# Layernorm channel sums by partition-folding DMAs and 64x64 matmul tiles, with halves abreast, in a transformer and ConvNeXt block kernel

## The chip, the core and the metric

The kernel runs on one core of one Trainium2 chip. A time is the device time of one execution in microseconds (us). The kernel before has a median of 3377.36 us over three runs (3374.6 to 3380.21). The profile is one further execution, recorded by the hardware profiler: that run took 3374.66 us, of which the profile's span covers 3372.8 us. Engines are named as in the profile: PE is TensorE, PEld its weight loads, DVE VectorE, ACT ScalarE, POOL GpSimd, SP SyncE.

## What is computed

Eight images of 384 channels and 32x32 = 1024 tokens, all float32, pass through two layers. In short form:

```python
# layer 0, per image: x is (1024 tokens, 384 channels)
xn  = layernorm(x, g1, beta1, eps=1e-5)            # ln1, over the channels
q, k, v = split(xn @ w_qkv.T + b_qkv)              # 8 heads of 48
x1  = x + concat(softmax(q k^T / sqrt(48)) v) @ w_proj.T + b_proj
xn2 = layernorm(x1, g2, beta2, eps=1e-5)           # ln2
x2  = x1 + gelu(xn2 @ w_fc1.T + b_fc1) @ w_fc2.T + b_fc2     # 384 -> 1536 -> 384
# layer 1, per image
y   = depthwise_conv_7x7(x2) + dw_b
y   = layernorm(y, ln_w, ln_b, eps=1e-6)           # ln3, over the channels
y   = gelu(y @ w1 + b1)                            # 384 -> 1536
gx  = sqrt(sum over tokens of y^2); nx = gx / (mean(gx) + 1e-6)
y   = grn_gamma * (y * nx) + grn_beta + y
out = x2 + y @ w2 + b2                             # 1536 -> 384
```

## The kernel before

**Layout.** Activations lie with channels on the partitions: an image is three tiles of 128 channels by 1024 tokens, and nearly every matmul has 512 tokens (half an image, "half 0" and "half 1") as its moving side. A layernorm is over channels, and so over the three tiles and over the 128 partitions of each.

**A layernorm** is the generator `layernorm` (L366). It works on one half: DVE adds the three channel tiles into one tile `a` of 128x512 (L379, L380); one PE matmul with a 128x128 tile of ones (L383) sums over the partitions and puts the sum on all 128 rows of a PSUM bank at once; three DVE operations subtract the mean (L387); ACT squares (L392); DVE adds the squares (L396, L397); a second matmul with ones (L400) gives the variance; ACT makes the reciprocal root (L408, L409); three DVE operations scale (L412). A float32 matmul is two passes of the array, so the profile counts each as two instructions. The `yield`s between the steps are waits of a planner, told of next.

**Order.** The program is written under a manual schedule: each engine executes its own queue in the order in which `main` (L1236 to L1387) writes it. The object `flow` keeps a clock of PE work as it is written (`flow.pe(us)`, 0.857 us for a 128x512 float32 matmul). Side chains, such as a layernorm, are generators started with `flow.spawn`; each `yield` gives the PE time after which the chain's next step is written. So a layernorm's steps fall between the matmuls of other work, and a `yield` that is too short for what precedes it leaves PE waiting at the layernorm's matmul, because everything later on PE is queued behind it.

**Stages of one image in the steady part**, about 407 us of PE time: `qk`; `attention`, 64 steps of a score and a product group, each of four 64-row tiles of the array; fc1 (384 to 1536) for half 0 and half 1; fc2 (1536 to 384) by `by_thirds` (L693), a fast block product of 15 products of four matmuls instead of 18; then, for the image before this one, `grn_up` (w1), the values of the next image, and `grn_down` (w2, `by_thirds` again). The 7x7 convolution runs on DVE the whole time.

**Where the layernorms are.** ln2 half 0 is spawned in the second half of attention (L593), right after the projection of half 0, with `spaced=True`; ln2 half 1 in the middle of fc1 (L679). At the start of fc2, `next_norms` (L1285) finishes the convolution and spawns ln3 of the image before as `abreast` (L414): both halves go step by step together, in `by_thirds`, with the yields stretched by 1.4. The second half takes its tiles from the four slots of `attn`, which is idle then. ln1 of the next image is spawned by `both` (L428), half 0 and then half 1, yields stretched by 1.8, 24 us after ln3 and so mostly in `grn_up`. Image 0 has its ln1 at the very start (L1243), and the last image has fc2 by halves and its ln3 in parts (L1310).

**POOL and its DMAs.** In `by_thirds` the function `adding` (L734) adds one 512 KB tile pair to another by an accumulating DMA issued from POOL (L736), and `difference` (L656) makes e tiles in the same way (L659). They are nearly all that POOL issues in the steady part. Weights stream on SP's queue.

## Time and profile before

| engine | busy us | share of span |
|---|---|---|
| PE (matmul) | 3323.2 | 99% |
| PEld (weight load, beside PE) | 1424.9 | 42% |
| DVE | 2551.5 | 76% |
| ACT | 1422.2 | 42% |
| POOL | 155.7 | 5% |

PE is busy in nearly all of the span, so what is between 3323.2 and 3372.8 us is start, end and a few waits. The granted PE clock is 0.996 of full speed on average. The sixteen DMA engines carry 275.79 MB, 82 GB/s on average, but unevenly: a `by_thirds` stage of an image in the middle (1401.38 to 1458.03 us) shows a DMA share of 0.66, the `grn_up` after it (to 1516.40 us) 0.33, and a piece of attention (1693 to 1700 us) 0.02. In those three pieces DVE is busy 48.40 of 56.65 us, 39.55 of 58.37 us and 6.96 of 7.00 us.

The page's rows for the groups of instructions give the line, the engine and operation, output and input tile, then the count, the busy time in us, the mean in ns, and the idle time before them with what ended it.

### The profile page before, as it was taken

The numbers are of one execution on the slowest core, as the hardware profiler recorded it, in microseconds if no ns is written. First come the engines' busy times: TensorE is split into PE (matmuls) and PEld (weight loads), VectorE is DVE, ScalarE is ACT, GpSimd is POOL, SyncE is SP. The second block draws the span as 40 slices with busy tenths as digits, with TensorE's granted clock in tenths as the row PEclk, the third lists the DMA queues.
The fourth block names the chain that finished last, engine by engine and source line by source line (L and its number), as shares of the span: only waits on it lengthen the run. The fifth ranks groups of instructions, "written<-read, shape, count | busy, mean of one in ns | idle before, by whom it ended". The sixth has DMA issues, their size and how long they took to land.

```text
span 3372.8 us, 36885 instructions
## 1 busy us (share of the span) xinstructions
PE 3323.2 (99%) x14122; PEld 1424.9 (42%) x14122; DVE 2551.5 (76%) x3089; ACT 1422.2 (42%) x1868; POOL 155.7 (5%) x181
## 2 busy tenths in 40 slices
PE   8999999999999999999999999999999999999999
PEld 3334434443344433444334443344434443344455
DVE  3345798877877878779787796976888779979950
ACT  2542353444534354343543525436254352531631
POOL 0202000000000000100001000010000000000000
PEclk9999999999999999999999999999999999999999
DMA  3427101542025410435005250052501633023231
GB/s 105 132 93 199 57 18 45 160 105 63 17 68 142 112 50 17 96 120 135 21 13 126 92 139 15 14 144 83 131 14 32 168 74 103 17 56 89 61 94 53
DMA packets 146024, 275.79 MB, mean 82 GB/s; under 512 B 34224, under 2 KB 36656, under 8 KB 145456
## 3 DMA queue, kind: packets, MB, share of 16 engines
q1 hardware_dynamic: 114416, 201.13, 19.3%
q0 software_dynamic: 30848, 69.74, 10.6%
q8 instruction: 114, 1.87, 0.2%
q10 hardware_dynamic: 576, 2.48, 0.2%
q14 instruction: 70, 0.57, 0.1%
HBM read 181.52 MB, written 33.82 MB: 64 GB/s over the span
## 4 chain that ended last, share of the span: by engine, by line
PE 83%; DVE 14%; DMA 1%; ACT 1%; issue 1%; SPq 0%; POOL 0%; DVEq 0%; ACTq 0%; POOLq 0%
PE s L547 12%; PE o L567 12%; PE fc L344 12%; PE fc_p L351 10%; PE h L351 10%; PE qk L331 6%; DVE acc L847 5%; PE v L476 4%; PE o L950 4%; PE proj L490 3%; PE o_p L351 3%; DVE wqkv L847 3%; PE h_last L994 2%; DVE y L727 1%; PE ln_var L400 1%; PE qk_last L344 1%
## 5 line engine op out<-in xcount | busy, mean ns | idle before, releaser
L847 DVE SCALAR_TENSOR_TENSOR acc<-pad,vec,acc 128x1024 f32<-128x1024 f32 x1008 | 1230.1, 1274 | 0.0
L556 ACT ACTIVATE p<-s 128x1024 f32<-128x1024 f32 x512 | 523.5, 1024 | 390.4 <-PE s L547 390.0
L547 PE MATMUL s<-qk 48*64 48x512 f32 x4096 | 537.4, 593 | 1.7 <-ACT qk L450 1.5
L567 PE MATMUL o<-p,v 64*64 64x512 f32 x4096 | 531.2, 590 | 0.0
L344 PE MATMUL fc<-xn,fc 128*128 128x512 f32 x1152 | 501.7, 593 | 1.2 <-DVE x L667 1.2
L344 PEld LDWEIGHTS fc<-xn,fc 128*128 128x128 f32 x1152 | 217.8, 190 | 278.5 <-issue 270.8
L351 PE MATMUL fc_p<-hid,fc 128*128 128x512 f32 x728 | 320.3, 592 | 0.0
L895 DVE TENSOR_TENSOR y<-h,y 128x512 f32<-128x512 f32 x288 | 198.4, 691 | 113.0 <-PE h L351 102.3
L351 PE MATMUL o_p<-y,w 128*128 128x512 f32 x624 | 274.4, 596 | 6.3 <-DVE y L727 6.3
L567 PEld LDWEIGHTS o<-p,v 64*64 64x64 f32 x4096 | 157.2, 133 | 285.3 <-issue 280.2
L363 ACT ACTIVATE hid<-fc,bfc_f 128x512 f32<-128x512 f32 x192 | 130.9, 686 | 348.2 <-PE fc L344 348.1
L547 PEld LDWEIGHTS s<-qk 48*64 48x64 f32 x4096 | 152.1, 133 | 295.6 <-issue 272.6
L351 PEld LDWEIGHTS fc_p<-hid,fc 128*128 128x128 f32 x728 | 138.3, 190 | 174.1 <-issue 169.3
L331 PE MATMUL qk<-xn,wqkv 128*128 128x512 f32 x480 | 207.4, 592 | 0.0
L351 PE MATMUL h<-acc,w_A 128*128 128x512 f32 x432 | 204.0, 592 | 0.0
L847 DVE SCALAR_TENSOR_TENSOR wqkv<-pad,vec,wqkv 128x416 f32<-128x416 f32 (+1 forms) x288 | 193.4, 745 | 0.6
L351 PEld LDWEIGHTS o_p<-y,w 128*128 128x128 f32 x624 | 117.8, 190 | 158.7 <-issue 128.3
L508 DVE TENSOR_TENSOR attn<-o,attn 128x512 f32<-128x512 f32 x64 | 44.0, 687 | 137.0 <-ACT attn L506 136.9
L450 ACT ACTIVATE qk<-qk,bqk 128x1024 f32<-128x1024 f32 x40 | 44.6, 1114 | 238.7 <-PE qk L331 238.7
L331 PEld LDWEIGHTS qk<-xn,wqkv 128*128 128x128 f32 x480 | 91.1, 190 | 114.1 <-issue 113.8
L476 PE MATMUL v<-wqkv,xn 128*128 128x384 f32 x384 | 128.6, 493 | 0.6 <-DVE xn L412 0.6
L490 PE MATMUL proj<-attn,wproj_sb 128*128 128x512 f32 x288 | 127.3, 595 | 0.8 <-DVE attn L534 0.8
(271 smaller groups left out, 3194.7 us busy)
## 6 DMA issues: line engine op xcount, KB each, us to landing
w_A<-in_w SPq DMA_DIRECT2D x72, 384.0 KB, 3.2
fc<-s_fc SPq DMA_DIRECT2D x91, 256.0 KB, 2.8
hid<-hid POOLq DMA_DIRECT2D x42, 512.0 KB, 6.8
fc<-in_wfc SPq DMA_DIRECT2D x54, 384.0 KB, 5.8
w<-s_w SPq DMA_DIRECT2D x78, 256.0 KB, 2.7
y<-y POOLq DMA_DIRECT2D x36, 512.0 KB, 7.3
xn<-in_x SPq DMA_DIRECT2D x16, 768.0 KB, 7.7
x<-in_x SPq DMA_DIRECT2D x16, 768.0 KB, 6.6
```

The costliest lines, as they stand in the source:

```text
L331: nc.tensor.matmul(out=ps[:, half(h)], lhsT=lhsT(k), rhs=rhs(k)[:, half(h)], start=(k == 0), stop=(k == nk - 1),)
L344: nc.tensor.matmul(out=ps, lhsT=lhsT(k), rhs=rhs(k)[:, half(h)], start=(k == 0), stop=(k == nk - 1))
L351: nc.tensor.matmul(out=bank, lhsT=lhsT, rhs=rhs, start=k == 0, stop=k == len(pairs) - 1)
L363: nc.scalar.activation(dst, src, function, **kw)
L476: nc.tensor.matmul(out=ps[:, :C], lhsT=xn[:, k, t * P : (t + 1) * P], rhs=wv_sb[:, k, :], start=(k == 0), stop=(k == CT - 1),)
L490: nc.tensor.matmul(out=ps, lhsT=wproj_sb[:, m, ct * P : (ct + 1) * P], rhs=attn[:, m, :], start=(m == 0), stop=(m == CT - 1),)
L547: nc.tensor.matmul(out=s[64 * i : 64 * i + 64, j, :], lhsT=kT[64 * j : 64 * j + HD, m, k0 : k0 + 64], rhs=qT[64 * j : 64 * j + HD, m, half ...
L556: nc.scalar.activation(p, s, AF.Exp)
L567: nc.tensor.matmul(out=outs[i][64 * j : 64 * j + 64, :], lhsT=v[keys, t, at : at + 64], rhs=p[keys, j, :], start=(t == 0), stop=(t == KT - 1),
L847: nc.vector.scalar_tensor_tensor(dst, window, tap, dst, ALU.mult, ALU.add)
L895: nc.vector.tensor_tensor(dst, bank, part, ALU.add)
L950: nc.tensor.matmul(out=ps, lhsT=tiles[k], rhs=y(k, part), start=(k == 0), stop=(k == HT - 1))
```

## The change

A new generator `token_sums` replaces the two matmuls with the 128x128 ones. Without `fold` it does what was done before. With `fold` 0 or 1, an accumulating DMA on POOL's queue first adds one half of the partitions of the 128x512 tile to the other (64 rows of 2 KB, 128 KB), the chain yields 3.4 us, and then two matmuls with 64x64 tiles of ones bring the sum of the 64 folded rows to the output's upper and lower 64 rows. Half 0 of the tokens folds into rows 0 to 63 and half 1 into rows 64 to 127, so that two halves abreast use all four 64x64 tiles of the array. With `fold="columns"`, for a half on its own, the left 256 columns are folded into the upper rows and the right 256 columns into the lower rows (two DMAs of 64 KB); the four tiles then have 256 columns each, the two column groups get a PSUM tile each, and the three subtractions of the mean become six of half width, the Ln one becomes two.

Folding is used in ln3 of images 0 to 6 and in ln1 of images 1 to 7 (halves abreast), and in ln2 half 0 of all eight images (columns). ln1 of image 0, ln2 half 1 and the last image's own ln3 keep the full sum. ln1 of images 1 to 7 goes from `both` to `abreast` with the factor 1.8; its delay after ln3 is 28 us instead of 24 (6 for image 1 as before), and its second half takes two "p" tiles of the pool `three` as places (image 1: `attn`, as ln3 does).

```diff
-    def layernorm(src, dst, h, eps, g, name, switch, spare=False, spaced=False, slow=1.0):
+    def token_sums(t, name, fold):
+        width = t.shape[-1]
+        if fold is None:
+            total = o_tile(name)[:, :width]
+            nc.tensor.matmul(out=total, lhsT=ones, rhs=t, start=True, stop=True)
+            flow.pe(U * width / NH)
+            return [(total, slice(0, width))]
+        rows = [slice(0, 64), slice(64, P)]
+        parts = [(fold, slice(0, width))]
+        if fold == "columns":
+            parts = [(j, slice(j * width // 2, (j + 1) * width // 2)) for j in range(2)]
+        for j, cols in parts:
+            nc.gpsimd.dma_start(out=t[rows[j], cols], in_=t[rows[1 - j], cols], accum_op=ALU.add)
+        yield 3.4
+        totals = []
+        for j, cols in parts:
+            total = o_tile(f"{name}_{j}")[:, : cols.stop - cols.start]
+            for i in rows:
+                nc.tensor.matmul(out=total[i, :], lhsT=ones[rows[j], :64], rhs=t[rows[j], cols], start=True, stop=True)
+            flow.pe(U * width / NH / 2)
+            totals.append((total, cols))
+        return totals
+
+    def layernorm(src, dst, h, eps, g, name, switch, spare=None, spaced=False, slow=1.0, fold=None):
...
         yield 2.6 * slow
-        total = o_tile(f"{name}_sum{h}")[:, :width]
-        nc.tensor.matmul(out=total, lhsT=ones, rhs=a, start=True, stop=True)
-        flow.pe(U * width / NH)
+        totals = yield from token_sums(a, f"{name}_sum{h}", fold)
         yield 0.8
         for ct in range(CT):
-            nc.vector.scalar_tensor_tensor(dst[:, ct, cols], total, -1.0 / C, src[:, ct, cols], ALU.mult, ALU.add)
+            for total, part in totals:
+                to, of = dst[:, ct, cols][:, part], src[:, ct, cols][:, part]
+                nc.vector.scalar_tensor_tensor(to, total, -1.0 / C, of, ALU.mult, ALU.add)
...
         yield 1.8 * slow
-        var = o_tile(f"{name}_var{h}")[:, :width]
-        nc.tensor.matmul(out=var, lhsT=ones, rhs=squares[0], start=True, stop=True)
-        flow.pe(U * width / NH)
+        totals = yield from token_sums(squares[0], f"{name}_var{h}", fold)
         yield 0.8
...
-        nc.scalar.activation(rstd, var, AF.Ln, bias=eps, scale=1.0 / C)
+        for var, part in totals:
+            nc.scalar.activation(rstd[:, part], var, AF.Ln, bias=eps, scale=1.0 / C)
...
-    def abreast(*args, parts=(0, 1)):
-        chains = [layernorm(*args[:2], h, *args[2:], spare=(h is parts[1])) for h in parts]
+    def averages():
+        return [attn[:, i, :] for i in range(4)]
+
+    def weight_places(name):
+        tiles = [three.tile([P, 2, NH], F32, tag="p", name=f"{name}_{i}") for i in range(2)]
+        return [t[:, j, :] for t in tiles for j in range(2)]
+
+    def abreast(*args, places=averages, fold=True, factor=1.4):
+        chains = [
+            layernorm(*args[:2], h, *args[2:], spare=places if h else None, fold=h if fold else None) for h in range(2)
+        ]
...
-                yield 1.4 * max(waits)
+                yield factor * max(waits)
...
-                ln = flow.spawn(layernorm(xt, xn, 0, eps0, "g2", f"ln2_{b}", False, spaced=True))
+                ln = flow.spawn(layernorm(xt, xn, 0, eps0, "g2", f"ln2_{b}", False, spaced=True, fold="columns"))
...
-        flow.finish(abreast(xn, xn, eps0, "g1", "ln1_0", False))
+        flow.finish(abreast(xn, xn, eps0, "g1", "ln1_0", False, fold=False))
...
-                state["norm1"] = flow.spawn(
-                    after(state["norm3"], both(xn, xn, eps0, "g1", f"ln1_{b + 1}", True, slow=1.8), 24 if b else 6)
-                )
+                name = f"ln1_{b + 1}"
+                places = (lambda: weight_places(name)) if b else averages
+                norm = abreast(xn, xn, eps0, "g1", name, True, places=places, factor=1.8)
+                state["norm1"] = flow.spawn(after(state["norm3"], norm, 28 if b else 6))
```

## The prediction, made before the changed kernel had run

> **What bounds the kernel now.** I read the busy row and the chain of waits on the page, then the rows of the two layernorm matmuls, then PE's waits.

> ```profile
> PE 3323.2 (99%) x14122; PEld 1424.9 (42%) x14122; DVE 2551.5 (76%) x3089; ACT 1422.2 (42%) x1868; POOL 155.7 (5%) x181
> ...
> PE 83%; DVE 14%; DMA 1%; ACT 1%; issue 1%; SPq 0%; POOL 0%; DVEq 0%; ACTq 0%; POOLq 0%
> ...
> L400 PE MATMUL ln_var<-ln_sq,ones 128*128 128x512 f32 (+3 forms) x82 | 43.8, 617 | 10.1 <-DVE ln_sq L397 10.1
> L383 PE MATMUL ln_sum<-ln_a,ones 128*128 128x512 f32 (+3 forms) x82 | 43.0, 606 | 9.2 <-DVE ln_a L380 9.2
> ```

> PE sets the end: removed PE time is gained unless a wait takes its place. DVE's share of the chain is start and end, where the last image's convolution runs by itself. The two rows' idle time (19.3 us) is mostly image 0 (gaps of 7.40, 4.34 and 3.38 us at its first sums, before any other work); from image 2 on, the layernorms cost almost no waiting. What a full sum costs, the timeline shows. In fc2, PE's rows:

> ```profile
> 1405.67 1.02 PE L383 MATMUL ln_sum<-ln_a,ones 128*128 128x512 f32 x2
> 1406.53 1.02 PE L383 MATMUL ln_sum<-attn,ones 128*128 128x512 f32 x2
> 1407.39 2.74 PE L351 MATMUL fc_p<-hid,fc 128*128 128x512 f32 x6
> ```

> Columns: start, duration, rows merged. Starts are 0.86 us apart: 0.86 for one sum, 1.72 for a pair, like any 128x512 matmul. In attention:

> ```profile
> 1695.09 0.69 DVE L380 TENSOR_TENSOR ln_a<-ln_a,x 128x512 f32<-128x512 f32 x1
> 1695.76 1.04 PE L567 MATMUL o<-p,v 64*64 64x512 f32 x8
> 1696.73 1.12 PE L383 MATMUL ln_sum<-ln_a,ones 128*128 128x512 f32 x2
> 1697.79 1.09 PE L547 MATMUL s<-qk 48*64 48x512 f32 x8
> 1698.69 1.04 PE L567 MATMUL o<-p,v 64*64 64x512 f32 x8
> ```

> Product groups start 1.72 apart without a sum (1694.04, 1695.76), here 2.93: the sum costs 1.21, its 0.86 and 0.35 for going from four tiles to one and back. Its input was ready at 1695.78, 0.95 before PE came.

> [...] attention's group of four, x8 with its two passes, takes 0.86, as one full matmul does, and the sum between such groups costs 0.35 more than itself. [...]

> ```profile
> hid<-hid POOLq DMA_DIRECT2D x42, 512.0 KB, 6.8
> fc_e<-hid POOLq DMA_DIRECT2D x14, 512.0 KB, 5.2
> qk<-qk SPq DMA_DIRECT2D x96, 64.0 KB, 2.3
> ```

> [...] I add 0.4 us for the second of two 64 KB folds.

> **The change, part by part.**

> *PE work.* ln2 half 0: 8 images, two sums each, 16 at 1.21 before. Afterwards four tiles of 256 columns among tiles of the same shape: half of 0.86 and a little for loads, 0.45. Gain 16 x 0.76 = 12.2 us. ln3 and ln1: 7 images, two pairs each, both: 28 pairs at 1.72. Afterwards 0.86 plus the 0.35 for leaving and re-entering the full array: 1.21; gain 28 x 0.51 = 14.3. Together 26.5 us. If the 256-column groups cost as much as 0.69 each, 3.8 less.

> *Work beside PE.* 88 DMAs, 8.8 MB on 275.79, and their issue on POOL (1.18 us for each 512 KB one, surely less here; POOL is 5% busy); DVE's mean subtractions in ln2 become six half-width operations of about 0.4 instead of three of 0.68, 0.3 us more per image, beside PE since DVE is 76% busy; one more Ln on ACT (42%). All hidden; bounds 0 and 1 us for each.

> *The latency of a fold, L,* from DVE's last addition to PE's start: [...] I take 2.8, and 2.4 for 64 KB; upper end 5.2, as if size didn't matter. Behind a fold's wait on PE stands everything PE has left.

> *ln3, six images in by_thirds* (the seventh goes by halves with wider gaps: nothing). In the built program's order, t counted from fc2's start: the sum group comes after 11 matmuls (9.4 to 10.6). The convolution ended long before (DVE waits 16.6 us for this sum in the trace), so the sum's folds are free. But the third product's last matmul now follows the sum group, and DVE has two operations on that product ahead of the mean subtractions: they end at 13.0. Six subtractions of 0.61: 16.7. Then one hid addition of 1.2, two e ones of 1.2 and an x one of 0.69: 20.9. The squares' additions (2 x 0.69 a half) end at 22.2 and 23.6. POOL issues the second fold then; its two earlier 512 KB adds were issued at 13.6 and 15.3. With 2.8 it lands at 26.4. PE arrives 16 matmuls after the sum group, at 24.4, and could lose nothing only with the second half there by about then: a stall of 2.0 to 2.2. 6 x 2.1 = 12.6 us. Bounds: nothing [...], and 4.5 each, 27, at L = 5.2.

> *ln1.* Half 1's sums, squares, scaling and DMA places move forward to half 0's; the steps issue nothing on SP before or after the change, and on POOL they pass the next by_thirds' adds, which start later. With the factor 1.8 the yield of 3.4 leaves 6.1 us of PE work for a fold; DVE adds 1 to 2 us of lead, having been done 0.77 to 3.19 before PE's arrival at ln1's groups in the trace: 7 to 8 us for L = 2.8. No stall for images 2 to 7. Image 1's (delay 6) folds stand on POOL behind the hid adds of its by_thirds: 0 to 2 us, against 2.0 that its half 1 waits now (1.83 and 0.21): nothing.

> *ln2 half 0.* The sum stands four pairs of attention after the projection, at +6.9 us; DVE is done at +2.65 in the usual image, the second 64 KB fold has landed at +5.6: 1.3 to spare. The variance has 3.6 us from DVE's end to PE, and needs 2.8: 0.8 to spare. In image 1 and in image 7 DVE is late already (gaps of 0.93 and 0.47 now at the variance): stalls of 1.5 and 1.0, together 2.5.

> *Sum.* 26.5 - 12.6 - 2.5 = 11.4, less 1 us for loads and issue: 10.4. Against the span of 3372.8: 3362.4. The three unprofiled runs' median stands 4.6 above that span: **3367 us**.

> **Rivals.** *No new wait* (0.20): the squares of ln3 come early enough[...]. For it: DVE had 16.6 us of slack at the sum. Against: the order puts DVE's two operations on the third product in front. 3377.4 - 26.5 + 3 = 3354.

> *The price of switching eats the gain* (0.10): [...] at 0.85 more instead of 0.35 the 28 groups gain nothing, and with ln3's wait only about ln2's 12.2 - 2.5 - 12.6 remains: 3380, no change.

> *Small folds are slow* (0.22), the other side: a 128x2 KB accumulation has a fixed price near the 5.2 us of the fastest 512 KB one, because adding in the DMA, not moving bytes, takes the time. Place: PE at ln3's variance and both ln2 groups. ln3 loses 6 x 4.5 = 27; ln2 loses 1.6 at the sum and 2.0 at the variance (5.6 needed, 1.3 and 0.8 spare at 2.4 + 0.4), 8 x 3.6 = 29, with 2.5 for images 1 and 7. 58 against 26.5: 3377.4 + 32 = 3409. It decides from about 1.2 us above my L: ln3 20, ln2 6 to 7, the gain is gone at 4.0 for 128 KB. For it: L736's median is 6.8. Against: those run while DMA is 0.66 busy; ln2's run at a share of 0.02.

> **Chances.** My forecast 0.48, with its own range 3359 to 3376; the others as given. 0.2% is 6.8 us, about what can be told from no change here. Faster than 3370.6: 0.8 of mine, all of the first rival, a little of the second: 0.61. Within: the rest of mine, most of the second, a few hundredths of the slow one's milder forms: 0.19. Slower: 0.20. The range 3350 to 3394 leaves out part of the first rival and the upper half of the slow one.

> **What would show it.** At PE's variance matmuls of ln3 a wait of about 2 us on a DMA, six times; at ln1 none; at ln2 about none but in images 1 and 7. Attention's product groups around a sum 2.2 apart instead of 2.93. A pair's place in fc2 1.2 wide. The row of 128 KB folds from POOL near 2.8 us, of 64 KB near 2.4. Wrong would be: folds over 4 us, DVE's squares before 20, or waits on folds in ln2 of every image.

## The result, and the profile after

The changed kernel takes 3412.96 us (median of four runs, 3408.96 to 3415.62), against 3377.02 us before: a ratio of 1.0105, 95% interval 1.0087 to 1.0122. It is slower by 36 us. The forecast was 3367, and the range 3350 to 3394 did not hold it. The profiled span is 3407.2 us, 34.4 more than before.

The page's busy row and PE's largest waits in the kernel after (columns of a wait: engine, line and waiting tile, what it waited for, us in total, times, longest us; L387 is the folded sum, L373 the full one):

```profile
PE 3322.6 (98%) x14330; PEld 1413.7 (41%) x14330; DVE 2549.8 (75%) x3113; ACT 1424.5 (42%) x1876; POOL 229.1 (7%) x269
```

```profile
PE ln_var L387 <- DMA ln_sq<-ln_sq: 14.0, 11, 3.6
PE fc_p L351 <- DVE hid L762: 9.2, 6, 1.5
PE ln_var L373 <- DVE ln_sq L423: 8.7, 9, 3.4
...
PE fc_p L351 <- issue: 7.7, 7, 1.7
...
PE h L351 <- DVE y L930: 5.6, 6, 0.9
```

Three groups of waits are new, with no such row among PE's waits in the kernel before: for the folds of a variance, for DVE's `hid` tiles in by_thirds (with the "issue" row beside it), and for DVE's `y` in grn_up. PE's busy time did not fall, although work was taken away. Passes of half rate and halves that no longer run together, both seen below, are part of the reason: in the run below that has neither in fc2 ("ln3's variance later") PE is busy 3309.3 us.

Where an image gained and lost shows in the stages of one in the middle, image 3. The views are busy times by window (columns: window, length, then busy time and instructions of PE, PEld, DVE, ACT and POOL, granted PE clock, DMA share, GB/s), first before, then after; the rows are fc2, grn_up and attention.

```profile
1401.38:1458.03 56.65, 56.65 (x134) 25.08 (x132) 48.40 (x67) 15.93 (x25) 7.08 (x6) 1.00 0.66 163
1458.03:1516.40 58.37, 58.37 (x138) 25.84 (x137) 39.55 (x59) 34.42 (x47) 0.00 (x0) 1.00 0.33 113
1617.95:1737.00 119.05, 119.05 (x1031) 42.37 (x1030) 88.79 (x93) 70.29 (x75) 0.00 (x0) 1.00 0.07 17
```

```profile
1415.26:1476.02 60.76, 57.02 (x138) 23.72 (x136) 43.68 (x60) 12.24 (x19) 10.49 (x10) 0.97 0.69 160
1476.02:1536.30 60.28, 59.35 (x149) 25.25 (x148) 43.72 (x66) 38.36 (x53) 1.62 (x2) 1.00 0.35 114
1637.86:1755.35 117.49, 117.49 (x1044) 42.28 (x1043) 88.67 (x96) 70.39 (x76) 3.33 (x4) 1.00 0.10 19
```

Attention, the window of the image after it, gives 1.57 us back. fc2 takes 4.11 more and grn_up 1.91 more, 4.45 in sum. From one `qk` to the next, images 2 to 5 take 411.1, 411.9, 410.8 and 412.4 us against 407.4, so the steady image costs 4.1 us more on average and the four 16.5. Images 0 and 1 together cost 11.8, image 6 4.8 and the last one 1.3: the 34.4 us.

The fc2 stage of image 3 in PE's timeline, after (start, duration, rows merged, in brackets idle before and what ended it):

```profile
1437.07 2.74 PE L351 MATMUL fc_p<-fc_e,fc 128*128 128x512 f32 x6
1441.25 1.08 PE L387 MATMUL ln_var<-ln_sq,ones 64*64 64x512 f32 x4 [1.44 <-DMA ln_sq<-ln_sq]
1442.09 1.07 PE L387 MATMUL ln_var<-attn,ones 64*64 64x512 f32 x4
1443.09 1.92 PE L351 MATMUL fc_p<-fc_e,fc 128*128 128x512 f32 x2
1444.80 18.28 PE L351 MATMUL fc_p<-hid,fc 128*128 128x512 f32 x40
1463.85 1.95 PE L351 MATMUL fc_p<-hid,fc 128*128 128x512 f32 x4 [0.77 <-issue]
1467.33 1.98 PE L351 MATMUL fc_p<-hid,fc 128*128 128x512 f32 x4 [1.53 <-DVE hid L762]
```

Four losses can be read here, each as the distance between starts less a matmul's own time:

- PE waits for the first variance fold: 1.60 us.
- The second half's fold lands 0.84 later, so the two halves run one after the other, and the group is 1.84 long instead of 0.86: 0.98.
- The first matmul after it starts at 1443.09 and the next at 1444.80, 1.71 later instead of 0.86. Its two passes (a pass is one of a matmul's two records: the page counts 4096 for the 2048 score matmuls) and the two after them take 0.854 us each instead of 0.428: 1.70. Such half-rate passes follow this wait in three images of six. They are not lost in full: fc2 takes 60.8, 60.8 and 61.3 us in these three (1, 3 and 5) and 60.0, 59.7 and 59.8 in the others, where the late stalls told of next are longer.
- About twenty microseconds later come two stalls, 0.93 and 1.70 us, for `hid` tiles from DVE: 2.63. (The view puts the first down to issue; DVE's `hid` addition before it ended 0.1 us earlier.)

With 0.37 that the sum's group of 64x64 tiles takes over its own passes (from 1424.27 to 1428.49 us with it and seven full passes, where nine at 0.428 would take 3.85) this makes 7.3, and smaller amounts bring it to 7.6 us over the 62 matmuls' worth of work that the stage now holds. Before, it held 66: the 60 of the product, four full sums of ln3 and two of ln1's half 0, which now runs later. 7.6 less the 3.43 of the four matmuls' worth that left is the 4.1 us lost.

ACT and DVE show where the late stalls come from. In ACT's timeline, first before and then after, look at the order of the Ln and of the copy of `x` into `pad`:

```profile
1417.03 0.69 ACT L408 ACTIVATE ln_rstd<-ln_var,eps 128x512 f32<-128x512 f32 x1 [4.66 <-PE ln_var L400]
...
1436.08 0.64 ACT L663 COPY pad<-x 128x512 f32<-128x512 f32 x1 [9.88 <-DVE x L727]
```

```profile
1452.09 0.63 ACT L698 COPY pad<-x 128x512 f32<-128x512 f32 x1 [14.23 <-DVE x L762]
...
1454.04 0.69 ACT L433 ACTIVATE ln_rstd<-ln_var,eps 128x512 f32<-128x512 f32 x1
```

DVE after:

```profile
1455.42 2.08 DVE L437 SCALAR_TENSOR_TENSOR acc<-acc,vec,ln_rstd 128x512 f32<-128x512 f32 x3 [2.70 <-ACT ln_rstd L434]
1457.41 2.07 DVE L437 SCALAR_TENSOR_TENSOR acc<-acc,vec,attn 128x512 f32<-128x512 f32 x3
...
1466.06 1.22 DVE L762 TENSOR_TENSOR hid<-hid 128x1024 f32<-128x1024 f32 x1
```

Before, the Ln waited for PE alone. After, the variance is on PSUM by 1443.1, but the Ln starts at 1454.04: in ACT's queue it now stands behind the copy of `x` into `pad`, and that copy waits for DVE, whose own work waits for the product that PE's wait has delayed. DVE then stands 2.70 us at the scaling of ln3, and the `hid` additions queued behind it reach PE too late (1467.33).

### The profile page after: what moved, and what is told of

It reads as the page before. It is cut to its first block, busy times and chain, and to the rows that moved or that the text cites. A ratio compares the mean times of both kernels' runs of the same rounds, so it can differ in the third digit from the quotient of the medians.

```text
span 3407.2 us, 37644 instructions
## 1 busy us (share of the span) xinstructions
PE 3322.6 (98%) x14330; PEld 1413.7 (41%) x14330; DVE 2549.8 (75%) x3113; ACT 1424.5 (42%) x1876; POOL 229.1 (7%) x269
## 5 line engine op out<-in xcount | busy, mean ns | idle before, releaser
L582 PE MATMUL s<-qk 48*64 48x512 f32 x4096 | 547.9, 595 | 4.6 <-ACT p L591 3.1
L602 PE MATMUL o<-p,v 64*64 64x512 f32 x4096 | 542.8, 593 | 0.0
L351 PE MATMUL fc_p<-hid,fc 128*128 128x512 f32 x728 | 325.1, 602 | 16.9 <-DVE hid L762 9.2
L351 PE MATMUL o_p<-y,w 128*128 128x512 f32 x624 | 274.5, 597 | 8.0 <-DVE y L762 8.0
L351 PEld LDWEIGHTS fc_p<-hid,fc 128*128 128x128 f32 x728 | 139.6, 194 | 201.5 <-issue 179.6
L351 PE MATMUL h<-acc,w_A 128*128 128x512 f32 x432 | 207.8, 596 | 5.6 <-DVE y L930 5.6
L351 PEld LDWEIGHTS o_p<-y,w 128*128 128x128 f32 x624 | 118.0, 191 | 160.2 <-issue 128.8
L698 ACT COPY pad<-x 128x512 f32<-128x512 f32 x48 | 30.0, 634 | 269.4 <-DVE x L762 212.9
L351 PEld LDWEIGHTS h<-acc,w_A 128*128 128x128 f32 x432 | 80.6, 190 | 115.0 <-issue 90.1
## 6 DMA issues: line engine op xcount, KB each, us to landing
hid<-hid POOLq DMA_DIRECT2D x42, 512.0 KB, 7.1
y<-y POOLq DMA_DIRECT2D x36, 512.0 KB, 7.2
```

Of the source, the lines that this page charges most:

```text
L351: nc.tensor.matmul(out=bank, lhsT=lhsT, rhs=rhs, start=k == 0, stop=k == len(pairs) - 1)
L582: nc.tensor.matmul(out=s[64 * i : 64 * i + 64, j, :], lhsT=kT[64 * j : 64 * j + HD, m, k0 : k0 + 64], rhs=qT[64 * j : 64 * j + HD, m, half ...
L602: nc.tensor.matmul(out=outs[i][64 * j : 64 * j + 64, :], lhsT=v[keys, t, at : at + 64], rhs=p[keys, j, :], start=(t == 0), stop=(t == KT - 1),
```

## The experiments

My theory after this reading: the folds in attention pay; the loss is made at ln3's variance in fc2 and by what follows from it, and in grn_up. The rival: folded sums cost in themselves, by switches of tiling, by the DMAs' latency or their traffic, wherever they stand. In the expectations the first is theory A and the second theory B, where nothing else is said. The diffs show the lines that matter, and comments in them are added.

### ln2 alone

```diff
-                norm = abreast(acc, acc, eps1, "lnw", f"ln3_{b - 1}", True)
+                norm = abreast(acc, acc, eps1, "lnw", f"ln3_{b - 1}", True, fold=False)
...
-                norm = abreast(xn, xn, eps0, "g1", name, True, places=places, factor=1.8)
-                state["norm1"] = flow.spawn(after(state["norm3"], norm, 28 if b else 6))
+                state["norm1"] = flow.spawn(
+                    after(state["norm3"], both(xn, xn, eps0, "g1", f"ln1_{b + 1}", True, slow=1.8), 24 if b else 6)
+                )
```

> Only ln2 half 0 is folded (columns); ln1 and ln3 stand as before. Theory A (the folds in attention pay, the loss is made in fc2 and grn_up): per image 1.57 us less in attention for images 2 to 6, 0.5 less in image 1, about 2 more in image 0 and in image 7, in sum 3371 to 3374 against 3377. Theory B (folded sums and their DMAs cost in themselves, wherever they stand): each of the eight images pays about 1.5 us or more, 3390.

Measured: 3374.37 us, ratio to before 0.9988 (0.9979 to 0.9997). Attention takes 117.49 us in images 2 to 5 as in the changed kernel, fc2 56.65 and grn_up 58.37 as before. The small gain of theory A is there; theory B's 3390 is excluded.

### ln3 full again

```diff
-                norm = abreast(acc, acc, eps1, "lnw", f"ln3_{b - 1}", True)
+                norm = abreast(acc, acc, eps1, "lnw", f"ln3_{b - 1}", True, fold=False)
```

> The changed kernel with ln3's sums full again (halves abreast, as before), ln1 and ln2 folded. Theory A: a fc2 stage of images 1 to 6 goes from about 60.4 to 55.0 us (60 matmuls and four full sums), 6 x 5.4 = 32 us less than the changed kernel: about 3380. Theory B: only a third of the added 36 us goes with ln3, about 3400.

Measured: 3383.01 us, 1.0016 (1.0009 to 1.0023). 30 us of the 36 go with ln3's folds, as theory A said. fc2 is 56.15 us and not 55.0: by this order it holds a part of ln1. What stays over the kernel before is mostly in images 0 and 1, 11.8 us together: the fc2 stage of image 0, which has no ln3, is 63.29 us long against 57.51. One loss of the steady image stays too, although PE no longer waits at ln3's variance: in grn_up PE waits for `y` as often and as long as in the changed kernel (5.6 us in six waits, 0.93 the longest).

### The Ln ahead of the pad copy

```diff
-        yield 0.8          # after the variance's matmuls
+        yield then         # 0.3 for ln3, else 0.8
```

> The changed kernel with one wait of ln3 shortened (the one after the variance, 0.8 to 0.3), so that Ln and Exp stand ahead of the pad copy in ACT's queue. Theory A: the two late stalls of fc2 (0.93 and 1.70 us over a matmul's time) go in six images, 6 x 2.6 = 16 us: about 3397; the wait at the variance stays. Theory B, or a late fold as the cause of those stalls: no change, 3413.

Measured: 3394.31 us, 1.0057 (1.004 to 1.0073): 18.7 us better than the changed kernel, where 16 was expected. ACT's timeline of this run at image 3:

```profile
1437.08 0.69 ACT L433 ACTIVATE ln_rstd<-ln_var,eps 128x512 f32<-128x512 f32 x1 [3.21 <-PE ln_var L387]
...
1446.03 0.63 ACT L700 COPY pad<-x 128x512 f32<-128x512 f32 x1 [6.36 <-DVE x L764]
```

The Ln now waits for PE alone and the copy comes after it. fc2 is 56.9 to 58.1 us in images 1 to 6 where it was 59.7 to 61.3. The order of two operations on ACT, an engine busy for 42% of the span, was worth half of the loss.

### ln3's sum earlier

```diff
-        yield 2.6 * slow
-        totals = yield from token_sums(a, f"{name}_sum{h}", fold)        # waits 3.4 for its folds
+        yield lead * slow                                                # 0.2 for ln3
+        totals = yield from token_sums(a, f"{name}_sum{h}", fold, sum_us)  # 1.0 for ln3
```

> The changed kernel with ln3's sum group after 3 matmuls of fc2 instead of 11 (its two first waits shortened; its folds have landed before fc2 starts in the trace), so that the mean subtractions go ahead of the operations on the third product and the squares end about 14 us into fc2. Theory A: the variance's wait, the halves apart and the half-rate passes after it go, and Ln comes ahead of the pad copy too: a fc2 stage of 53.9 us (60 matmuls and two groups of 1.24), 6.4 us less in six images, 38 us: about 3375. Theory B (folds are slow by themselves, 3.4 us and more): the wait at the variance stays at 1 to 1.5 us and fc2 comes to 56 or more: 3388.

Measured: 3370.94 us, 0.9979 (0.9971 to 0.9987): 42 us better than the changed kernel, and now faster than before. PE's timeline at the variance:

```profile
1416.53 6.17 PE L351 MATMUL fc_p<-hid,fc 128*128 128x512 f32 x14
1422.63 0.65 PE L387 MATMUL ln_var<-ln_sq,ones 64*64 64x512 f32 x2
1422.64 0.65 PE L387 MATMUL ln_var<-attn,ones 64*64 64x512 f32 x2
1423.11 0.59 PE L387 MATMUL ln_var<-ln_sq,ones 64*64 64x512 f32 x2
1423.12 0.60 PE L387 MATMUL ln_var<-attn,ones 64*64 64x512 f32 x2
1423.65 4.56 PE L351 MATMUL fc_p<-hid,fc 128*128 128x512 f32 x10
```

No wait, and the four tiles start 10 ns apart in this view: the group is 1.02 long from its start to the next matmul. fc2 takes 55.15 us (the 53.9 expected and a group of ln1 that now falls into it) and grn_up 58.08; its wait for `y` has gone too: ln1, which starts when ln3 has ended, now falls at another place. The steady image is 404.06 us, 3.3 less than before. The folds are the same as in the changed kernel; only their places differ. Theory B falls.

### ln3's variance later

```diff
-        totals = yield from token_sums(squares[0], f"{name}_var{h}", fold)         # waits 3.4
+        totals = yield from token_sums(squares[0], f"{name}_var{h}", fold, var_us)   # 5.6 for ln3
```

> The changed kernel with the plan's wait for ln3's variance folds at 5.6 instead of 3.4: PE comes 4 matmuls later, and the Ln still stands behind a pad copy in ACT's queue. Theory A (two separate losses): the wait at the variance, the halves apart and the half-rate passes go (3.4 us in six images, 20 us), the late stalls stay: 3393. Theory B (the late stalls follow from the wait at the variance): both go, 3377.

Measured: 3368.34 us, 0.9972 (0.996 to 0.9984). Here my expectation was the wrong one. I took the wait at the variance and the late stalls for two separate losses; the wait went, and of the late stalls all but a few tenths of a microsecond, with the Ln still behind a pad copy (in image 3 the copy at 1437.72 and the Ln at 1439.67). fc2 is 54.5 us in images 2 to 5, and grn_up, which now holds all of ln1, 59.4, without the wait for `y`. The wait and the late stalls stand in one chain. In the changed kernel the wait, the halves apart and the half-rate passes put PE 4.3 us back in image 3, and 2.3 in image 4, which has no half-rate passes; DVE's operations on the next products start as much later, so does the pad copy, and the Ln behind it. Each of the two links can be cut: without the delay the copy is early enough, and with the Ln ahead of it the delay does not pass on.

### Image 1's ln1

```diff
+                if b == 0:
+                    norm = both(xn, xn, eps0, "g1", name, True, slow=1.8)
+                else:
+                    norm = abreast(xn, xn, eps0, "g1", name, True, places=places, factor=1.8)
```

> The run with ln3's early sum, and image 1's ln1 alone as in the kernel before (one half after the other, full sums). It parts what the run e5 put right at once. Theory A: the fc2 stage of image 0 goes back from 63.4 to 57.5 us: 3365; the rest of e5's 12 us stands in ln2 of images 0 and 7 and in the last image's ln3. Theory B: image 0 loses in its ln2 half 0, and fc2 was only where it showed: 3370.

Measured: 3364.01 us, 0.9963 (0.9952 to 0.9974), 7 us under the run with the early sum, to which this edit is added; by the two ratios it is 5, and their intervals overlap a little. The fc2 stage of image 0 goes from 63.4 to 58.3 us. In the changed kernel the variance folds of this ln1 stood on POOL behind 512 KB additions, two of which were still under way, and landed 6.8 and 6.5 us after their issue; PE waited 3.63 us for them.

### The folds kept where they pay

```diff
-                ln = flow.spawn(layernorm(xt, xn, 0, eps0, "g2", f"ln2_{b}", False, spaced=True, fold="columns"))
+                ln = flow.spawn(layernorm(xt, xn, 0, eps0, "g2", f"ln2_{b}", False, spaced=True, fold="columns" if 0 < b < B - 1 else None))
...
-                norm = abreast(acc, acc, eps1, "lnw", f"ln3_{b - 1}", True)
+                norm = abreast(acc, acc, eps1, "lnw", f"ln3_{b - 1}", True, **({} if b == B - 1 else dict(lead=0.2, sum_us=1.0)))
```

ln3's sum is early except in the last image, ln2 is folded in images 1 to 6 only, and image 1's ln1 is as in the run above.

> As the run with ln3's early sum, but the folds are left out where they stood badly: ln1 of image 1 as in the kernel before, ln2 half 0 full in images 0 and 7, ln3 in the last image with its old waits. Theory A: the steady image keeps its 404.1 us (407.4 before), six times 3.3 = 20 us, and the start and end lose nothing: 3357. Theory B: what the early sum won comes from shifting the same waits to start and end, which are then bound elsewhere: 3368 or more.

Measured: 3359.06 us (3357.49 to 3361.52), 0.9948 (0.9932 to 0.9965). This version beats both kernels, by 18 us and by 54 us. A second run asks what ln1's folds are worth in it.

> As the run before it, but ln1 of every image as in the kernel before (halves one after the other, full sums). Theory A: without a stall ln1's folding gains 0.96 us an image (two pairs of 1.71 for two groups of 1.24), so this one is 6 us slower than the run before it: 3363. Theory B: halves abreast in ln1 bring a wait of DVE in grn_up that costs what the fold gains: the same time, 3357, or less.

Measured with ln1 as before throughout: 3362.62 us, 0.9961 (0.9947 to 0.9975). Where nothing stalls, ln1's folds are worth about 3.6 us by the medians, somewhat under the 6 expected; the two intervals overlap, though the runs themselves do not (3361.52 at most against 3362.16 at least), so the sign is clear and the size is not settled.

### Half-rate passes without folds

```diff
 # the kernel before; ln3 only
-        yield 1.8 * slow       # between the squares' additions and the variance
+        yield 0.0
```

> The kernel before, full sums throughout, with only the wait ahead of ln3's variance taken out of the plan (1.8 to 0), so that PE comes to the full sum about 2 us before its squares are added. It asks whether the half-rate passes after a wait need the folds. Theory A (they follow any wait of PE of 1 to 2 us, not always): 1.9 us of waits and up to 1.7 us of half-rate passes in six images, 3388 to 3396, with half-rate passes in one or more of the six. Theory B (they come from four-tile groups within full-array work): waits alone, 3388, and no half-rate pass.

> As e7 (full sums throughout), with ln3's variance one matmul earlier still, so that PE waits about 2.1 us instead of 1.2. In e7 no wait was followed by half-rate passes. Theory A (the length of the wait decides, folds or not): half-rate passes follow in two or more of six, 3398 to 3406. Theory B (they need the half-filled four-tile group after the wait): none, 6 x 3.4 = 20 us of waits, 3397.

In the second of these the wait ahead of the squares' additions is also 0.7 instead of 1.8. Measured: 3392.35 us, 1.0049 (1.0033 to 1.0065), with waits of 1.23 us and no half-rate pass in fc2; then 3411.32 us, 1.0105 (1.0085 to 1.0125), with waits of 2.09 us and half-rate passes in all six images. PE's timeline in the second:

```profile
1425.91 1.12 PE L400 MATMUL ln_var<-ln_sq,ones 128*128 128x512 f32 x2 [2.09 <-DVE ln_sq L397]
1427.31 2.07 PE L400 MATMUL ln_var<-attn,ones 128*128 128x512 f32 x2 [0.27 <-DVE attn L397]
1429.18 1.81 PE L351 MATMUL fc_p<-fc_e,fc 128*128 128x512 f32 x2
1430.82 2.74 PE L351 MATMUL fc_p<-hid,fc 128*128 128x512 f32 x6
```

The matmul at 1429.18 takes 1.64 until the next, not 0.86. Both runs have full sums only, so here the half rate came without a fold and without a small tile, after the waits of 2.09 us and not after those of 1.23. 0.86 us more of wait cost 19 us in six images, 3.2 us each. In the changed kernel the waits were 1.02 to 1.44 us and the half rate came in three of six, so the length of the wait does not decide alone. The first group after the wait also uses only two of the four tiles there (1.84 us for both halves in image 3). The last section sets both this and the moment of the wait beside the clock's records.

### A fold without its addition

```diff
-            nc.gpsimd.dma_start(out=t[rows[j], cols], in_=t[rows[1 - j], cols], accum_op=ALU.add)
+            nc.gpsimd.dma_start(out=t[rows[j], cols], in_=t[rows[1 - j], cols])
```

> The changed kernel with the folds as plain copies of the same 128 and 64 KB: the addition in the DMA is left out. It asks what of a fold's latency is the addition. Theory A (a fold's time is the fixed price of a small transfer and its company): landings as in the changed kernel, 2.3 and 2.6 us in attention and 2.7 to 3.5 us at ln3's variance. Theory B (the addition takes the time): 0.5 us and more off each, and the waits at ln3's variance gone.

Measured in one run: 3402.64 us. POOL's row for ln2's folds of the squares (size, median us to landing), after and then in this run:

```profile
ln_sq<-ln_sq POOLq DMA_DIRECT2D x16, 64.0 KB, 2.6
```

```profile
ln_sq<-ln_sq POOLq DMA_DIRECT2D x16, 64.0 KB, 1.9
```

In quiet attention the addition takes 0.4 to 0.7 us of a fold (1.9 each as copies; as additions 2.3 for the first and 2.6 for the second), and it adds about 0.3 us to the issue on POOL (0.52 against 0.81). At ln3's variance the first copy still lands after 3.3 to 3.65 us, no earlier than the addition did (2.9 to 3.5), and the second after 2.2 to 2.6 (2.7 to 3.2). The waits there remain, so neither theory was right in full: the addition has a price, but not the one that decided.

## Why the prediction was wrong

**PE work: right.** A folded sum in attention takes 0.43 us of the stream, between groups that start at 1719.11 and 1720.40 us, against 0.45 forecast; attention gained 1.57 us an image, forecast 1.52. Among full-array matmuls the sum's group in image 3 cost 0.37 over its own passes, forecast 0.35. The rival, with 0.85, is out.

**The latency of a fold: size off for 128 KB.** From DVE's last addition to PE's start it was 3.9 and 3.4 us at ln3's variance of image 3; I had taken 2.8, an estimate; no transfer of this size stood in the trace before (a line from the 2.3 of its 64 KB transfers on SP's queue to the 5.2 of its faster 512 KB additions would give 2.7). The landings are 3.5 and 2.95 us after the issue, and the issue comes 0.3 us after DVE. Elsewhere 128 KB took longer still: the folds of ln1 in images 2 to 7 landed after 3.5 to 5.2 us, those of ln3's sum in images 2 to 6 after 4.8 to 6.3. My sign of being wrong, folds over 4 us, was met there, though PE did not wait for these. In attention my 2.4 and the 0.4 for the second, estimates too, compare with 2.3 and 2.6 measured. (The folds' traffic is 9.4 MB and not the 8.8 I gave, and a fold has 64 rows of 2 KB and not the 128 that the slow rival names; nothing hangs on either.)

**ln3's wait: right in place and nearly in size.** Squares were forecast at 22.2 and 23.6 us into fc2 and came at 22.05 and 23.4; PE was forecast at 24.4 and came there. The stall was forecast at 2.1; the wait and the halves apart make 2.6.

**"All hidden", and "ln1 ... No stall": these failed.** My sum let an image gain 1.5 us: 1.52 in attention and 2.04 in the four pairs, less a wait of 2.1 at ln3's variance that ends with itself. It did not end there. In image 3, 2.6 us of late stalls followed through DVE, the pad copy and the Ln, and 1.7 us of half-rate passes, which came in three images of six. I had followed the order on PE, DVE and POOL around the variance and not what stands ahead of the Ln in ACT's queue. The runs with the early sum and with the late variance show it: with the wait gone, these go. A third term, a wait of 1.1 us for `y` in grn_up, has a cause of its own, since it stays in the run with ln3 full, where ln3 has no wait. With ln1's halves abreast its six scalings stand on DVE in one stretch (1503.16 to 1507.21), ahead of the `y` for which PE waits until 1507.87; I had asked of ln1 only whether its folds would land in time. It comes and goes with ln1's place. The three terms are 5.4 us, more than image 3's net loss of 4.5; without them the image would have gained 0.9 us.

**Image 1's ln1: failed.** I set nothing for it, with its folds named as standing behind the additions on POOL. They landed 6.5 and 6.8 us after their issue, PE waited 3.63 us where 0 to 2 had been put, the fc2 stage of image 0 lost 5.1 us, and the run that took these folds out won 5 to 7.

**ln2 in images 1 and 7.** Image 1 gained 0.5 us in attention, about as forecast. Image 7 lost 3.8 in attention where a gain of 1.52 less a stall of 1.0 was put, and 2.3 of it came back in the stages after. What varies most is image 0's attention: it ended 3 us apart between runs in which it had the same work, so nothing is read from it.

**The slow rival** named 3409, and 3413 came, but it was not what happened. Its mechanism was 5.2 us for a fold and 29 us lost in ln2; at these places the folds landed 2.3 to 3.5 us after their issue, and ln2 alone gained 3 us. Its latency was met only where PE did not wait for it, and in image 1's ln1.

## What to carry to other kernels

A wait on an engine at its limit had a price beyond its length here (PE, 98% busy: in image 3 a wait of 1.44 us for the first fold, and fc2 4.11 us longer): follow what the delayed engine feeds, on every queue, until something is shown to absorb it, and look above all at which operation stands ahead of the one that ends the wait. When work is moved onto a path with more latency, give it the time in the plan, by an earlier start or by a longer gap. ln3's sum 8 matmuls earlier and ln3's variance 4 matmuls later turned the same folds from 36 us lost into 6 and 8 us won, and these runs do not tell the two ways apart. The folds kept only where they stood well won 18.

## What the runs showed of the hardware

```profile
1439.88:1443.29 3.41, 2.04 (x9) 0.65 (x10) 0.00 (x0) 0.00 (x0) 2.38 (x2) 1.00 0.87 147
1443.29:1446.70 3.41, 3.41 (x5) 1.35 (x5) 1.58 (x2) 0.00 (x0) 0.00 (x0) 0.50 1.11 189
```

```profile
2241.58:2244.99 3.41, 1.91 (x5) 0.70 (x5) 3.20 (x5) 0.84 (x2) 0.00 (x0) 1.00 0.27 77
2244.99:2248.40 3.41, 3.41 (x10) 1.50 (x9) 3.41 (x5) 1.79 (x3) 0.90 (x1) 1.00 0.02 5
```

PE was busy longer in the first step of the first pair (2.04 us against 1.91), and yet only there did the half clock follow. But 1.84 us of that step went to groups that fill two of the four tiles. An estimate from the traces counts each pass with its 0.428 us for 512 columns and with the share of the array that its tile covers: the step was filled to 0.31 in the changed kernel and to 0.41 in the other run. Over all 13 traces, from 25 us after the start, 92 of the 92 full-clock steps filled by this estimate to less than 0.385 were followed by a half-clock step, 11 of the 26 from there to 0.42, and 1 of the 12493 above; in the traces of the two kernels alone it is 16 of 16, 1 of 3 and none of 1928.

So in these traces the half clock went with how full a step was by this estimate, and with it how much of a wait fell into one step. What sets the clock was not shown, and no run was made to move a wait within a step. Two images of the changed kernel take 241 steps (822.6 us), which puts the wait at the same moment of a step in every second image: it lay within one step in images 1, 3 and 5 (filled to 0.36, 0.31 and 0.24) and was divided over two in the others (0.50 and more). In the second run under "Half-rate passes without folds" one image takes 121 steps, so its six waits of 2.09 us all lie at the same moment of a step (0.25 to 0.29); they are one case seen six times, and a wait of 2.09 us divided over two steps was not tried. In image 1 of the changed kernel a wait of 1.05 us, with the half-filled groups after it, was followed by a half-clock step.
